# Block 1's attention contexts on tiles of 64 rows and 32 columns of the matmul array

## The chip, the core and the metric

The kernel runs on one NeuronCore of a Trainium2 chip. A core has five engines, each with a queue of its own that it works through in order: TensorE (PE, the 128x128 matmul array, whose results go to PSUM), VectorE (DVE), ScalarE (ACT), GpSimd (POOL) and SyncE (SP, which issues the DMAs here). PSUM has eight banks; a tile `[128, 512]` of float32 fills one. The metric is the time of one execution in microseconds (us), the median of several runs.

## What is computed

The input `x` has 32 sequences of 64 tokens with 512 channels. Two transformer blocks run one after the other, in float32:

```python
# block 0: 8 query heads of 64, 1 key/value head, rope, softmax over all 64 keys, gated MLP of 2048
x = res + ctx @ Wo.T
x = x + silu(h @ Wg.T) * (h @ Wu.T) @ Wd.T

# block 1: layer norm with scale and shift, 16 query heads of 32, 4 key/value heads from a latent of 128
q = (h @ Wq.T).reshape(B, T, 16, 32).transpose(0, 2, 1, 3)
c_kv = h @ Wkd.T
k = (c_kv @ Wku.T).reshape(B, T, 4, 32).transpose(0, 2, 1, 3)
v = (c_kv @ Wvu.T).reshape(B, T, 4, 32).transpose(0, 2, 1, 3)
k_exp = jnp.repeat(k, 4, axis=1)
v_exp = jnp.repeat(v, 4, axis=1)
attn = softmax(rope(q) @ rope(k_exp).T / sqrt(32))   # 64 tokens: the mask hides nothing
y = attn @ v_exp                                      # the "contexts" that the change rearranges
out = x + y.transpose(0, 2, 1, 3).reshape(B, T, 512) @ Wo.T
```

So in block 1 four query heads share one key/value head (a "group"), and there are four groups, numbered g = 0 to 3. In the kernel g = 2m + r, with m and r each 0 or 1.

## The kernel before

The 2048 tokens are cut into eight units of 256 tokens, four sequences each. A unit passes through block 0's attention (`attention0`), the MLP (`mlp`, with seven products in place of eight for each pair of 2x2 blocks), and block 1's attention (`attention1`). Generators stand for these, and `Order` interleaves their pieces: while TensorE works on the MLP of unit u, pieces of `attention0` of unit u+1 and `attention1` of unit u-1 are put between. Below that, the compiler's scheduler gives each engine its final order of instructions and gives each PSUM tile a bank, from the banks that it reckons to come free first. At the start (list `FIRST`) and at the end (list `LAST`) the order on TensorE is written out by hand. At the end nothing is left of the MLP, and `attention1` of the units 6 and 7 runs alone.

What the change touches lies in `attention1`:

- `keys_values` (L855 on) makes keys and values of the unit. The keys go to `kb` with a mask, twice for each sequence: in copy r only the channels of the group r of a pair stay, the rest is zero. The values of a sequence go to `vb` in block-diagonal form: rows 0 to 63 (the 64 keys) hold the 32 channels of r = 0, rows 64 to 127 hold those of r = 1 in the next 32 columns, and the rest is zero. Eight copies on ACT (L883) write them; the zeros were written once, by `early` (L1093) for the two buffers `vblk1`, and by a memset (L1204) for unit 7's own.
- `scores(t)` (two sequences at a time, t = 0 or 1) makes a bank of scores for each m, with the columns in the order (head j, copy r, key), on tiles of 64 rows and 64 columns of the array. `softmax` works on each bank, `turn` turns the result with TensorE transposes (`turned`, L600) and copies it to `pT` (L601, ACT).
- `context(t, pTs)` multiplies: for a sequence b of the two and a pair m, one matmul of all 128 rows (64 keys of r = 0 and 64 of r = 1) and 64 columns (32 channels of each), over 4 x 64 = 256 moving columns. Four such matmuls fill one bank, `cx`; two copies (L951 on ACT; for unit 7 the second on DVE, L949) bring it to `cT`, and `output` multiplies that by `wo1` (`po`, L565).

A float32 matmul shows in the trace as two matmul records. The products of the MLP are L977 (`gu`) and L1036 (`down`).

Of the kernel before, what the change touches and what calls it, by code (L numbers as in the profile page):

```python
# [17 lines left out]
P = 128  # L18
B, S, D = 32, 64, 512
T = B * S  # L20
KC = D // P
UT = 256
US = UT // S
# [5 lines left out]
HD1, HALF1 = 32, 16  # L29
# [15 lines left out]
TURN = (0.15911865234375, 3.628432750701904e-05, 6.4192136051133275e-09, 1.4247115856860781e-12)  # L45
ROUND = 12582912.0
WARM = 11
STAY = 14104
FIRST = "aaaaaaa bb a mm aa bb a bbb aa b mm a bb r aa a m b a bi m b i a | b".replace(" ", "")
EARLY = 4  # L50

# [1 line left out]
TWO_PI = float(np.nextafter(np.float32(2 * np.pi), np.float32(0)))  # L53


C_COND, C_VECS, C_CS1, C_MASK, C_FREQ = 0, KC * B, KC * B + 16, KC * B + 16 + 2 * S, KC * B + 18 + 2 * S
C_SIGN, C_ALL = C_FREQ + 1, C_FREQ + 2

OTHER = [(i + HALF1) % 32 for i in range(32)]
# [67 lines left out]
def two_blocks(ctx: ExitStack, tc: tile.TileContext, a: dict, out: bass.AP):  # L127
    nc = tc.nc
# [8 lines left out]
    def bank(tag, name):  # L137
        return psum.tile([P, 512], F32, tag=tag, name=name, bufs=BANKS[tag])
# [4 lines left out]
    def abank(name):  # L143
        tags = homes["now"]
        homes["n"] += 1
        return bank(tags[homes["n"] % len(tags)], name)


    stays = {"all": const.tile([P, STAY], F32, tag="stays", name="stays"), "at": 0}

    def fixed(shape):
        n, i = int(np.prod(shape[1:])), stays["at"]
        stays["at"] += n
        assert stays["at"] <= STAY
        t = stays["all"][:, i : i + n]
        if len(shape) == 2:
            return t
        names = "abc"[: len(shape) - 1]
        return t.rearrange(f"p ({' '.join(names)}) -> p {' '.join(names)}", **dict(zip(names, shape[1:])))

    def work(tag, shape, name, bufs=2):
        return wk.tile(shape, F32, tag=tag, name=name, bufs=bufs)
# [19 lines left out]
    for q in range(US):  # L182
        rows = slice(q * HALF0, (q + 1) * HALF0)
        for i in range(2):
            block = ident[rows, rows][:, i * HALF1 : (i + 1) * HALF1].unsqueeze(1).unsqueeze(1)
            to = spread[rows, q].rearrange("p (r a h f) -> p r a h f", r=2, a=2, h=2)[:, :, i]
# [24 lines left out]
    kmask = small[:, C_MASK:C_FREQ]  # L211
# [5 lines left out]

    vblk0 = [fixed([P, US, HD0]) for i in range(2)]

    vblk1 = [fixed([P, US, 2, 2 * HD1]) for i in range(2)]  # L220

    s0a = fixed([P, KC, B])
    s0b = fixed([P, KC, B])
# [225 lines left out]
    def tables_by_quarters(u, few, room):  # L449

        r = few[:, 0]
        nc.vector.tensor_tensor(
            few[:, 1:3], angle[:, :, u * S : (u + 1) * S], r.unsqueeze(1).to_broadcast([P, 2, S]), ALU.mult
        )
        ps = abank(f"tab_{u}").rearrange("p (i b s) -> p i b s", i=2, s=S)
        spread_out(ps, few[:, 1:3])
        pr = abank(f"row_{u}")[:, :UT]
        spread_out(pr.rearrange("p (b s) -> p b s", s=S), r)
        cs = work("cs", [P, 2, UT], f"cs_{u}", 1)
        ps = ps.rearrange("p i b s -> p i (b s)")  # L460
        nc.scalar.copy(cs[:, 0], ps[:, 0])
        nc.scalar.mul(cs[:, 1], ps[:, 1], sign_of)
        row = space(room, "r", UT, f"r_a{u}")
        nc.scalar.copy(row[HD0:], pr[HD0:])
        return cs[:, 0], cs[:, 1], row
# [22 lines left out]
    def tile4(room, tag, name):  # L488
        return space(room, tag, KC * UT, name).rearrange("p (c t) -> p c t", t=UT)
# [33 lines left out]
    def root_row(parts, eps, room, name):  # L523

        r = space(room, "r", UT, f"r_{name}")[:, :S]
        root_by_quarters(parts, eps, r, f"qs_{name}")
        yield 0.5, 1.0
        pr = abank(f"row_{name}")[:, :UT]
        spread_out(pr.rearrange("p (b s) -> p b s", s=S), r)
        return pr  # L530
# [94 lines left out]

    mlp_in = {}

    def attention0(u, room, early=None, late=None):
        kb, vb = kblk0[u % 2], vblk0[u % 2]
        lean = "lean" in room  # L630
        h = tile4(room, "h", f"h0_{u}")
# [14 lines left out]
        def keys_values():  # L646
            kv = abank(f"kv0_{u}")
            project(kv[:, :UT], wqkv[0], slice(2 * P, 3 * P), h)
            return kv

        norm = rms(u, s0a, h, room, f"a{u}")
        yield next(norm)
        if early:
            early()
        r = yield from norm
        kv, turn = None, None
        if lean:
            few = space(room, "few", 3 * S, f"quarters_{u}").rearrange("p (k c) -> p k c", c=S)
            if u == 0:

                idle(4)
                kv = keys_values()
            root_by_quarters(r, eps0, few[:, 0], f"ms_a{u}")
            kv = kv or keys_values()
# [4 lines left out]
        if lean:  # L669
            cos, sin, r = tables_by_quarters(u, few, room)  # L670
# [9 lines left out]
        kv = kv or keys_values()  # L680
# [36 lines left out]
        for ts in ((0,), (1,)) if lean else ((0, 1),):  # L717
            banks = [abank(f"sc0_{u}_{ts[0]}_{r}")[:, : 256 * len(ts)] for r in range(2)]
            for n in range(KC * len(ts)):
                t, c = ts[n // KC], n % KC  # L720
                for b in range(2):
                    cols = slice((2 * t + b) * S, (2 * t + b + 1) * S)
                    for r, sc in enumerate(banks):
# [5 lines left out]
                            start=True,  # L729
                            stop=True,  # L730
                        )
            p = ps[ts[0]] if lean else both
# [3 lines left out]
        cT = tile4(room, "h", f"cT0_{u}")  # L736
        pTs = []
# [34 lines left out]
        r = yield from rms(u, s0b, h, room, f"b{u}")  # L772
        if lean:
# [4 lines left out]
            r = abank(f"row_b{u}")[:, :UT]  # L778
# [14 lines left out]


    def attention1(u, room):
        vb = room.get("vb", vblk1[u % 2])
        x = x_units[u]
        lean = "lean" in room
        early = "early" in room
# [20 lines left out]
        if slim:  # L820
            r = yield from root_row(parts, eps1, room, f"c{u}")
        else:
            r = space(room, "r", UT, f"r_c{u}")
# [33 lines left out]
        def keys_values():  # L857
            kv = abank(f"kv1_{u}")
            nc.tensor.matmul(kv[:, :UT], wkv1[:, 0], latT, start=True, stop=True)
            for t in range(2):  # L860
                nc.tensor.matmul(
                    kv[:, UT + t * P : UT + (t + 1) * P], latT[:, t * P : (t + 1) * P], wkv1[:, 1], start=True, stop=True
                )
            kr = space(room, "kr", UT, f"kr_{u}").rearrange("p (b s) -> p b s", s=S)
            few = [P, US, S]
            rotate(
                kr,
                kv[:, :UT].rearrange("p (b s) -> p b s", s=S),
                cos.unsqueeze(1).to_broadcast(few),
                sin.unsqueeze(1).to_broadcast(few),  # L870
                few,
                f"k1_{u}",
            )
            kb = space(room, "kb", 2 * UT, f"kb1_{u}").rearrange("p (b g s) -> p b g s", b=US, g=2)
            wide = [P, US, 2, S]
            mask = kmask.unsqueeze(1).unsqueeze(3).to_broadcast(wide)
            nc.gpsimd.tensor_tensor(kb, kr.unsqueeze(2).to_broadcast(wide), mask, ALU.mult)
            for t in range(2):
                for b in range(2):
                    v = kv[b * S : (b + 1) * S, UT + t * P : UT + (t + 1) * P]  # L880
                    v = v.rearrange("p (m r d) -> p m r d", m=2, r=2)
                    for r in range(2):
                        nc.scalar.copy(  # L883
                            vb[r * S : (r + 1) * S, 2 * t + b, :, r * HD1 : (r + 1) * HD1], v[:, :, r, :]
                        )
            return kb

        queries = [query(i) for i in range(2)]
# [14 lines left out]
        cT = tile4(room, "h", f"cT1_{u}")  # L903
# [29 lines left out]
            return pTs  # L933

        def context(t, pTs):
            cx = abank(f"cx1_{u}_{t}").rearrange("p (b c s) -> p b c s", b=2, c=KC)
            for b in range(2):
                for m in range(2):
                    nc.tensor.matmul(  # L939
                        cx[m * S : (m + 1) * S, b],  # L940
                        vb[:, 2 * t + b, m, :],
                        pTs[m][:, :, b * S : (b + 1) * S],
                        start=True,
                        stop=True,
                    )
            to = cT[:, :, t * P : (t + 1) * P].rearrange("p c (b s) -> p b c s", s=S)
            for b in range(2):
                if slim and b:
                    nc.vector.tensor_copy(to[:, b], cx[:, b])  # L949
                else:  # L950
                    nc.scalar.copy(to[:, b], cx[:, b])  # L951

        ps = []
        for t in range(2):
# [3 lines left out]
            if not lean:  # L958
                pTs = yield from turn(t, ps[t])
                context(t, pTs)  # L960
                yield 1.0, 1.5 * t
        if lean:
            pTs = []
# [125 lines left out]
            if i == 1:  # L1089
                load_sets(MW)  # L1090

    def early():
        for z in vblk1:  # L1093
            nc.gpsimd.memset(z, 0.0)

    def second(u, room=None):
        room = room or {"ring": "1"}
        while u not in finished:
# [17 lines left out]
    first = work("p0", [P, 1024], "p0_0", 1)  # L1116

    def later_angles():
# [2 lines left out]

    ahead = Job(attention0(1, {"ring": "1", "lean": True}, late=later_angles), A0)
    streams = {
        "a": attention0(0, {"ring": "0", "lean": True, "p": [first[:, :512], first[:, 512:]]}, early),
        "b": ahead.pieces,
        "m": other_mods(),
    }
# [28 lines left out]
    def spare(tag, cols, name, bufs=2):  # L1156
        return work(tag, [P, cols], f"own_{name}", bufs)
# [5 lines left out]
        "ring": "0",  # L1163
        "lean": True,
        "early": True,
        "vb": vblk1[0],
        "p": [t[:, j * 512 : (j + 1) * 512] for t in two for j in range(2)],
        "latT": [few[:, :UT]],
        "kr": [few[:, UT:]],
# [15 lines left out]
    for u in range(NU):  # L1185
# [14 lines left out]
        rest = order.run(jobs, until=tuple(must))  # L1200
    order.run([*rest, Job(down(NU * NP - 1), 3.0)])
    homes["now"] = everywhere
    zeros = spare("pT1", 512, "vb7", 2).rearrange("p (b r d) -> p b r d", b=US, r=2)
    nc.gpsimd.memset(zeros, 0.0)  # L1204
    big = [spare("mw", 1792, f"mw{j}", MW) for j in range(4)]
    room7 = {
        "ring": "-",
        "lean": True,
        "vb": zeros,
        "h": [big[0][:, :1024], big[1][:, :1024], big[1][:, :1024]],  # L1210
        "latT": [big[0][:, 1024:1280]],
        "kr": [big[0][:, 1280:1536]],
# [95 lines left out]
```

## Time and profile before

| what | value |
|---|---|
| median of 3 runs | 1032.84 us (1032.0 to 1033.85) |
| the profiled execution | 1034.73 us, its span from first to last instruction 1032.7 us |
| mean granted TensorE clock | 0.996 |
| DVE, POOL, ACT busy | 547.4, 437.4, 332.2 us |
| block 1's contexts on TensorE (L939) | 128 records of 128 rows x 64 columns, 256 moving columns |
| block 0's contexts on TensorE (L746) | 128 records of 64 x 64, 256 moving columns |
| value copies to `vb` (L883, ACT) | 64 of 206 ns |
| memsets for the zeros (L1094, L1204, POOL) | 3 of 524 ns, at 1.8, 13.0 and 949.1 us |

A line of the timeline reads: start in us, duration in us, engine, source line, operation, out<-in, tile of the array (rows * columns), shape, number of records merged into the line. The duration of a merged line runs to the modelled end of its last record, which lies after the next line's start, because matmuls are pipelined. What a stretch takes of TensorE is therefore read from the start of one line to the start of the next.

### The profile page before, as it was taken

Reading aid. Unit: us, or ns where it says so; the run is one execution under the profiler, and the core shown is the slowest. Engines: PE = TensorE matmul, PEld = TensorE weight load, DVE = VectorE, ACT = ScalarE, POOL = GpSimd, SP = SyncE. Lnnn points to the kernel's source line nnn. Section 1 sums busy time; section 2 is a strip of 40 time slices with the busy share of each in tenths; the row PEclk is TensorE's granted clock in tenths of the full one; section 3 lists DMA queues with packets and bytes.
Section 4 is the critical chain, followed back from the end, with each engine's and each line's share of the span. In section 5 each row is a group of like instructions: output and inputs, shape, how many; then the busy total and the mean of one; then the engine's idle time right before and its main releaser. Section 6 shows DMA issues by size and latency. Waiting matters only on the chain.

```text
span 1032.7 us, 21599 instructions
## 1 busy us (share of the span) xinstructions
PE 1004.3 (97%) x8598; PEld 935.9 (91%) x8598; DVE 547.4 (53%) x1376; ACT 332.2 (32%) x684; POOL 437.4 (42%) x522
## 2 busy tenths in 40 slices
PE   8999899999999999999999999999999999999997
PEld 7789899998999988989999989899999899999986
DVE  5766855535355485343664366652565525553374
ACT  4432113345114243142340342242333522334042
POOL 5335446344254442345342454324563243643351
PEclk9999999999999999999999999999999999999999
DMA  9736896363665364672646646447754547666201
GB/s 322 260 128 227 269 328 242 116 215 128 235 214 203 122 224 151 217 259 101 235 149 228 235 143 213 156 149 240 247 182 161 186 166 258 215 215 215 92 1 41
DMA packets 68850, 198.53 MB, mean 192 GB/s; under 512 B 7312, under 2 KB 16272, under 8 KB 68368
## 3 DMA queue, kind: packets, MB, share of 16 engines
q1 hardware_dynamic: 68752, 197.17, 55.2%
q8 instruction: 68, 1.11, 0.4%
q14 instruction: 30, 0.25, 0.1%
HBM read 180.37 MB, written 16.78 MB: 191 GB/s over the span
## 4 chain that ended last, share of the span: by engine, by line
PE 84%; DVE 6%; POOL 4%; DMA 2%; issue 2%; ACT 1%; SPq 0%; POOLq 0%; DVEq 0%; ACTq 0%
PE gu L977 34%; PE down L1036 17%; PE q L565 11%; PE po L565 9%; PE sc L912 2%; PE pp L600 2%; PE cx L939 2%; PE lat L565 1%; DMA set<-in_wmlp 1%; PE kv L565 1%; PE sc L725 1%; PE cx L746 1%; PE tab L436 1%; DMA mod<-in_mod 1%; DVE sm L593 1%
## 5 line engine op out<-in xcount | busy, mean ns | idle before, releaser
L977 PE MATMUL gu<-h,set 128*128 128x128 f32 x2048 | 288.1, 277 | 10.2 <-DVE c L996 5.6
L977 PEld LDWEIGHTS gu<-h,set 128*128 128x128 f32 x2048 | 259.1, 192 | 19.3 <-issue 13.0
L977 PE MATMUL gu<-hc,set 128*128 128x128 f32 x1536 | 215.7, 276 | 0.0
L977 PEld LDWEIGHTS gu<-hc,set 128*128 128x128 f32 x1536 | 194.0, 193 | 1.1 <-issue 0.6
L1015 POOL TENSOR_TENSOR act<-c,c 128x384 f32<-128x384 f32 x64 | 66.5, 1039 | 198.2 <-DVE c L1003 141.8
L1036 PE MATMUL down<-td,set 128*128 128x128 f32 x1024 | 137.7, 276 | 2.5 <-POOL td L1018 2.5
L1036 PEld LDWEIGHTS down<-td,set 128*128 128x128 f32 x1024 | 125.6, 192 | 4.2 <-POOL td L1018 3.4
L989 ACT COPY e<-gu 128x128 f32<-128x128 f32 x128 | 33.7, 264 | 261.0 <-PE gu L977 246.9
L1003 DVE TENSOR_TENSOR c<-gu,u 128x256 f32<-128x256 f32 x128 | 53.4, 419 | 106.5 <-PE gu L977 106.0
L1036 PE MATMUL down<-act,set 128*128 128x128 f32 x768 | 109.6, 278 | 0.0
L565 PE MATMUL q<-h,stays 128*128 128x256 f32 x480 | 109.1, 380 | 0.0
L565 PE MATMUL po<-cT,stays 128*128 128x256 f32 x480 | 108.3, 380 | 0.7 <-ACT cT L756 0.7
L991 DVE TENSOR_TENSOR u<-e,gu 128x128 f32<-128x128 f32 x128 | 36.0, 281 | 129.9 <-ACT e L989 129.1
L1036 PEld LDWEIGHTS down<-act,set 128*128 128x128 f32 x768 | 97.8, 192 | 5.3 <-issue 3.2
L565 PEld LDWEIGHTS q<-h,stays 128*128 128x128 f32 x480 | 89.5, 190 | 12.1 <-issue 0.4
L565 PEld LDWEIGHTS po<-cT,stays 128*128 128x128 f32 x480 | 89.2, 190 | 12.0 <-ACT cT L756 0.8
L595 POOL TENSOR_TENSOR p<-p,sm 128x512 f32<-128x512 f32 x40 | 41.3, 1050 | 121.0 <-DVE sm L594 113.7
L576 POOL TENSOR_TENSOR qT<-u_q,v_q 128x512 f32<-128x512 f32 x30 | 38.1, 1270 | 85.8 <-DVE v_q L575 85.7
L1072 ACT ACT_TABLE_LOAD x35 | 44.9, 1283 | 54.9 <-DVE c L1003 54.4
L621 DVE TENSOR_TENSOR x<-x,po 128x512 f32<-128x512 f32 x28 | 19.2, 687 | 72.8 <-PE po L565 72.8
L1017 POOL TENSOR_TENSOR td<-act 128x256 f32<-128x256 f32 x64 | 46.8, 732 | 5.6 <-DVE act L1014 0.9
L1072 ACT ACTIVATE c<-gu 128x128 f32<-128x128 f32 x64 | 17.7, 277 | 86.2 <-DVE c L1003 82.4
(267 smaller groups left out, 1335.7 us busy)
## 6 DMA issues: line engine op xcount, KB each, us to landing
set<-sums SPq DMA_DIRECT2D x168, 512.0 KB, 5.5
set<-in_wmlp SPq DMA_DIRECT2D x192, 384.0 KB, 4.4
sums<-set SPq DMA_DIRECT2D x24, 512.0 KB, 4.4
x<-in_x SPq DMA_DIRECT2D x8, 512.0 KB, 6.4
mod<-in_mod SPq DMA_DIRECT2D x7, 512.0 KB, 7.1
a<-in_wmlp SPq DMA_DIRECT2D x24, 128.0 KB, 3.2
out_x<-x SPq DMA_DIRECT2D x12, 256.0 KB, 2.5
stays<-in_wo SPq DMA_DIRECT2D x2, 1024.0 KB, 10.8
```

What stands on the lines that cost most here:

```text
L565: nc.tensor.matmul(ps, w[:, k, cols], h[:, k, :], start=(k == 0), stop=(k == KC - 1))
L576: nc.gpsimd.tensor_tensor(dst, u, v, ALU.add)
L595: nc.gpsimd.tensor_tensor(p8, p8, sm.unsqueeze(2).to_broadcast(wide), ALU.mult)
L600: nc.tensor.transpose(pp[:, c, :], p[:, c * P : (c + 1) * P], ident)
L977: nc.tensor.matmul(ps, w[:, slot, k * P : (k + 1) * P], b[of][:, k], start=start and k == 0, stop=k == 1, skip_group_check=True)
L989: nc.scalar.copy(e, ps[:, 0])
L991: nc.vector.tensor_tensor(u2, e, ps[:, 1], ALU.add)
L1003: nc.vector.tensor_tensor(c.rearrange("p (a b) t -> p a b t", b=2)[:, :, 1], ps[:, 2:4], u2.unsqueeze(1).to_broadcast([P, 2, HT]), ALU.add,)
L1015: nc.gpsimd.tensor_tensor(act[:, 1:4], gate[:, 1:4], c[:, 1:4], ALU.mult)
L1017: nc.gpsimd.tensor_tensor(td[:, 0:2], act[:, 1:3], act[:, 0:2], ALU.subtract)
L1036: nc.tensor.matmul(sums_of[u][p][:, c], w[:, slot, c * P : (c + 1) * P], b[of], start=q % NP == 0 and i % 2 == 0 and c == 0, stop=q % NP = ...
L1072: nc.scalar.activation(gate[2][:, 0], gate[0][:, 0], AF.Silu)
```

## The change

The values lose their zeros. `vb` of a sequence has 32 columns for each m, and its 128 rows hold r = 0 and r = 1: in the order (0, 1) for the sequence b = 0, and (1, 0) for b = 1. The mask of the keys gets the same turn, so that the keys' copies of each second sequence stand in the order (1, 0). A context is then one matmul for each sequence, m and r: 64 rows (the half where this r lies) and 32 columns (at position 32 g). There are eight in place of four for a t, on eight different tiles of the array, and each sequence has a bank of its own. The copies to `vb` are four in place of eight, each of 64 x 128 elements. Three memsets go, and so does unit 7's own buffer.

```diff
-    vblk1 = [fixed([P, US, 2, 2 * HD1]) for i in range(2)]
+    vblk1 = [fixed([P, US, 2, HD1]) for i in range(2)]
...
-        vb = room.get("vb", vblk1[u % 2])
+        vb = vblk1[u % 2]
...
-            mask = kmask.unsqueeze(1).unsqueeze(3).to_broadcast(wide)
+            mask = kmask.rearrange("p (b g) -> p b g", g=2).unsqueeze(3).to_broadcast(wide)
             nc.gpsimd.tensor_tensor(kb, kr.unsqueeze(2).to_broadcast(wide), mask, ALU.mult)
-            for t in range(2):
-                for b in range(2):
-                    v = kv[b * S : (b + 1) * S, UT + t * P : UT + (t + 1) * P]
-                    v = v.rearrange("p (m r d) -> p m r d", m=2, r=2)
-                    for r in range(2):
-                        nc.scalar.copy(
-                            vb[r * S : (r + 1) * S, 2 * t + b, :, r * HD1 : (r + 1) * HD1], v[:, :, r, :]
-                        )
+            v = kv[:, UT:].rearrange("p (t m r d) -> p t m r d", t=2, m=2, r=2)
+            for b in range(2):
+                for r in range(2):
+                    rows = slice((r ^ b) * S, (r ^ b) * S + S)
+                    nc.scalar.copy(
+                        vb.rearrange("p (t b) m d -> p b t m d", b=2)[rows, b], v[b * S : (b + 1) * S, :, :, r]
+                    )
...
         def context(t, pTs):
-            cx = abank(f"cx1_{u}_{t}").rearrange("p (b c s) -> p b c s", b=2, c=KC)
-            for b in range(2):
-                for m in range(2):
-                    nc.tensor.matmul(
-                        cx[m * S : (m + 1) * S, b],
-                        vb[:, 2 * t + b, m, :],
-                        pTs[m][:, :, b * S : (b + 1) * S],
-                        start=True,
-                        stop=True,
-                    )
-            to = cT[:, :, t * P : (t + 1) * P].rearrange("p c (b s) -> p b c s", s=S)
-            for b in range(2):
+            banks = [abank(f"cx1_{u}_{t}_{b}")[:, :UT].rearrange("p (c s) -> p c s", s=S) for b in range(2)]
+            for m in range(2):
+                for r in range(2):
+                    for b, cx in enumerate(banks):
+                        rows, g = slice((r ^ b) * S, (r ^ b) * S + S), 2 * m + r
+                        nc.tensor.matmul(
+                            cx[g * HD1 : (g + 1) * HD1],
+                            vb[rows, 2 * t + b, m],
+                            pTs[m][rows, :, b * S : (b + 1) * S],
+                            start=True,
+                            stop=True,
+                        )
+            for b, cx in enumerate(banks):
+                to = cT[:, :, t * P + b * S : t * P + (b + 1) * S]
                 if slim and b:
-                    nc.vector.tensor_copy(to[:, b], cx[:, b])
+                    nc.vector.tensor_copy(to, cx)
                 else:
-                    nc.scalar.copy(to[:, b], cx[:, b])
...
-    def early():
-        for z in vblk1:
-            nc.gpsimd.memset(z, 0.0)
...
-    zeros = spare("pT1", 512, "vb7", 2).rearrange("p (b r d) -> p b r d", b=US, r=2)
-    nc.gpsimd.memset(zeros, 0.0)
...
-    mask = (np.arange(P)[:, None] % 64 // HD1 == np.arange(2)).astype(np.float32)
+    mask = (np.arange(P)[:, None] % 64 // HD1 == np.array([0, 1, 1, 0] * 2)).astype(np.float32)
```

## The prediction, made before the changed kernel ran

> **What bounds the kernel now.** I read the page's head and busy times first: TensorE is busy in nearly all of the span, at full clock, and no other engine passes 53%.
>
> ```profile
> span 1032.7 us, 21599 instructions
> PE 1004.3 (97%) x8598; PEld 935.9 (91%) x8598; DVE 547.4 (53%) x1376; ACT 332.2 (32%) x684; POOL 437.4 (42%) x522
> PE 84%; DVE 6%; POOL 4%; DMA 2%; issue 2%; ACT 1%; SPq 0%; POOLq 0%; DVEq 0%; ACTq 0%
> ```
>
> The third line is the chain of waits: 84% of the span is TensorE's own work. So a microsecond less on TensorE is a microsecond less of time, except in stretches where TensorE waits. From the sums by stretch, TensorE idles 5.8 us of 220 in 200–420, 3.3 of 240 in 420–660, 0.1 of 170 in 660–830, 1.25 of 155 in 830–985. Next, the timeline of TensorE around a context of block 1 and a context of block 0:
>
> ```profile
> 394.04 1.08 PE L939 MATMUL cx<-pT,stays 128*64 128x256 f32 x8
> 395.05 0.71 PE L977 MATMUL gu<-h,set 128*128 128x128 f32 x4
> ...
> 336.56 1.09 PE L746 MATMUL cx<-pT,stays 64*64 64x256 f32 x16
> 337.59 0.71 PE L1036 MATMUL down<-act,set 128*128 128x128 f32 x4
> ```
>
> From start to next start, block 1's eight records take 1.01 us and block 0's sixteen take 1.03. All stream 256 columns; a full-array record of that width takes 0.216 us (the groups' `po` L565, 16 records in 3.46 us). So records on different tiles run side by side: eight on two tiles are four waves, sixteen on four tiles also four. A context costs 0.15 + 0.216 per wave. Unit 6 agrees: sixteen records on two tiles, eight waves, run from 1005.40 to the next line at 1007.31: 1.91 us, against 0.15 + 8 x 0.216 = 1.88. In one wave the single starts lie 7 ns apart.
>
> **The change: contexts.** Now sixteen records go to eight tiles. If all eight run side by side: two waves, 0.15 + 2 x 0.216 + 6 more starts of 7 ns = 0.62 us, 0.39 less. The trace shows no eight at once. It shows two row halves with two column groups (L746 above), and one row group with four column groups (L330, 32 records of 128 columns from 27.79, first three pitches 7, 6, 7 ns, waves of 109 ns). Both at once is new, and so is a bank written from both row halves: block 0 gives each row half its own bank. Bounds: two waves (-0.39), or one record after another, sixteen waves, 3.6 us (+2.6). I take two waves: neither four column streams nor two row halves slowed a wave in those rows, and the two halves write different partitions of the bank.
>
> [...]
>
> Places, by the order in which the changed program's instructions stand on TensorE. Eight contexts of units 0 to 5 stand whole: 8 x -0.39 = -3.1. The second contexts of units 2 and 4 are cut into two runs of four, a bank each, with `down` products between: 2 x (0.15 + 0.43 + 0.02) + 0.10 for one more change of tiling (a first tiled record starts 0.205 after the last full one, a usual pitch is 0.112) = 1.30 against 1.01: +0.29 each, +0.6. The first contexts of units 3 and 4 were cut before (0.58 + 1.01) and are cut into two and six matmuls now (0.58 + 0.62): -0.39 each, -0.8. Sum -3.3.
>
> **Scores get another order.** They take 1.03 us when the two banks alternate, more when one bank's matmuls come first:
>
> ```profile
> 362.69 1.10 PE L912 MATMUL sc<-kb,qT 64*64 64x128 f32 x32
> 363.72 1.05 PE L1036 MATMUL down<-act,set 128*128 128x128 f32 x7
> ...
> 811.06 1.09 PE L912 MATMUL sc<-kb,qT 64*64 64x128 f32 x16
> 812.08 0.71 PE L1036 MATMUL down<-act,set 128*128 128x128 f32 x4
> 812.63 0.39 PE L1036 MATMUL down<-td,set 128*128 128x128 f32 x2
> 812.94 1.09 PE L912 MATMUL sc<-kb,qT 64*64 64x128 f32 x16
> 813.96 0.49 PE L1036 MATMUL down<-td,set 128*128 128x128 f32 x2
> ...
> 685.61 1.97 PE L725 MATMUL sc<-stays,qT 64*64 64x64 f32 x64
> 687.50 0.71 PE L1036 MATMUL down<-act,set 128*128 128x128 f32 x4
> ```
>
> Unit 4's second scores stand as two halves (1.02 + 1.02); in the changed program they alternate: -1.0. Block 0's scores of unit 6 (1.89) alternate after four; with the alternating price of 1.09 (L725 at 318.96), 0.1 for another change of tiling and 0.28 for the second bank (the two copies from `cx` at 377.11 start 0.27 apart): 1.47, -0.4. In units 1, 2 and 5 (1.30 before) two `gu` products now stand between contexts and scores, and both score banks are just-used context banks (unit 2 excepted): 1.03 + 0.28 + 0.1, about 0, from -0.2 to +0.3 each. Sum -1.4.
>
> **New waits.** A context takes two banks, so scores wait for two ACT copies in place of fewer. A copy starts 0.04 after the context's last modelled end (377.07) and takes 0.38; the last record starts 0.32 after the first and lasts 0.38. So the banks are free about 1.1 and 1.4 us after the context's start. TensorE, at 0.62, first does two `gu` products (four records, 0.54 with the tiling change): 1.15, just covered for the first bank. Behind a waiting score stands all of TensorE's queue. ACT idled 1.17 us before those copies, so I add nothing; without that cover a table load (1.28) in front costs that much in each of three places.
>
> **Where gains are lost.** In unit 1 DVE is back to back from 376 to 390 with angles and softmax, and TensorE waits for it:
>
> ```profile
> 386.08 0.44 PE L600 MATMUL pp<-stays,p 128*128 128x128 f32 x2 [0.81 <-POOL p L595]
> 388.32 1.13 PE L977 MATMUL gu<-h,set 128*128 128x128 f32 x8 [1.80 <-DVE c L996]
> ```
>
> What the context at 375.94 saves becomes a longer wait here: 0.4 lost, and I allow 0.2 more for the other waiting stretch (602, 1.67 us). +0.6.
>
> **The tail.** Nothing covers it:
>
> ```profile
> 1020.63 0.37 ACT L951 COPY own_mw<-cx 128x256 f32<-128x256 f32 x1 [0.49 <-PE cx L939]
> 1021.04 0.42 DVE L949 COPY own_mw<-cx 128x256 f32<-128x256 f32 x1 [3.44 <-ACT own_mw L951]
> 1021.44 0.37 ACT L951 COPY own_mw<-cx 128x256 f32<-128x256 f32 x1 [0.44 <-PE cx L939]
> 1021.85 0.42 DVE L949 COPY own_mw<-cx 128x256 f32<-128x256 f32 x1 [0.38 <-ACT own_mw L951]
> 1022.33 7.17 PE L565 MATMUL po<-own_mw,stays 128*128 128x256 f32 x32 [0.93 <-DVE own_mw L949]
> ```
>
> The DVE copy of the same bank waits for ACT's. With two banks the program lets it wait for TensorE alone. Unit 7: contexts start at 1019.45; the last `pT` copy ends at 1020.14, so the last four matmuls run from 1020.20, their second records start by 1020.50 and end by 1020.87; both copies run from 0.10 after, to 1021.40; `po` starts at 1021.46: -0.87. Unit 6: its last `pT` lands at 1006.25, so the last records start by 1006.53 and scores at 1006.84, not 1007.31: -0.47. Sum -1.3.
>
> **The rest costs nothing.** Value copies on ACT: eight of 206 ns become four of about 260 (between 206 for 64x64 and 366 for 64x256): -0.6 us of ACT per unit, where ACT idles two thirds; the queue behind gains nothing on the path. The memsets at 1.8 and 13.0 lie under TensorE's waits for DMA and for products of POOL that end before 13.0; the one at 949.1 is followed by no wait of TensorE. The key mask keeps its shape, 128x512; no DMA is added.
>
> **Sum.** -3.3 - 1.4 + 0.6 - 1.3 = -5.4 us. The profiled execution took 1034.73 in all, 2.0 of it outside its span of 1032.7; the median is 1032.84, near this span, and I take the difference from the median: 1027.4. Bounds of this case: the losses could double and the scores bring nothing (1029.8), or nothing is lost and units 1, 2, 5 gain 0.2 each (1026.2); with half a microsecond of run-to-run spread, 1025.7 to 1030.3.
>
> **Rivals.**
> (1) The change doesn't do what it says: four at once, each row half and bank apart. Whole contexts keep four waves (0), runs of four in one bank take four waves each (2 x (2 x 1.01 + 0.1 - 1.01) = +2.2), the two that were cut +0.2 each, scores -1.4, parallel copies in the tail -0.4: about 1033.7. For it: no row shows a bank shared by row halves. Against: the different partitions.
> (2) Slower: in each context a matmul that meets a busy bank holds the queue, so only two run at once. Eight waves, 1.88 us, +0.87 for each of sixteen contexts: +13.9; the scores' -1.4 and the copies' -0.4 stay: 1044.9. It decides from six waves per context on (16 x 0.43 = +6.9, against -1.8). For it: in the scores at 213.18 five matmuls of one bank ran in pairs before those of the other bank began, though on other rows. Against: in unit 0's context at 233.00 one column group went on while the other still waited for its `pT`.
> (3) The waits for the two banks: table loads or MLP copies on ACT stand before the context copies, about 1.3 us in three places: 1031.3. For it: ACT is in order, and a table load came right after the copies at 377.77. Against: the idle 1.17 us.
>
> **How the numbers follow.** The forecast gets 0.68, rival (1) 0.09, rival (2) 0.13, rival (3) 0.10. What a measurement can tell from no change is about 0.2%, 2.1 us: faster means under 1030.8. The forecast lies there, and (3) about half: faster 0.73. Same: (1) and the rest of (3): 0.13. Slower: (2), and (1) if a little worse: 0.14. The forecast's own range would hold under 0.6; it is carried over (3) and (1): 1025.0 to 1033.8.
>
> **What would show it.** Right: contexts of sixteen records in 0.62 us from start to next start, starts 7 ns apart eight at a time; unit 4's second scores at 1.03; in the tail ACT and DVE copies side by side and `po` about 0.9 us sooner after the contexts' start; TensorE's waits at 386 and 388 longer. Wrong: contexts of 1.0 us (rival 1) or 1.9 (rival 2); waits of scores for ACT `cT` (rival 3). A slower loop of DVE or POOL in the MLP, which I do not expect, would also break the sum.

## The result, and the profile after

| | kernel before | changed kernel |
|---|---|---|
| median | 1032.53 us (1030.47 to 1034.56, 6 runs) | 1026.80 us (1025.15 to 1028.28, 6 runs) |
| ratio of the times | | 0.9939, 95% interval 0.9926 to 0.9952 |
| profiled execution, span | 1034.73, 1032.7 us | 1028.28, 1026.3 us |
| contexts of block 1 (L939), start to the next kind's start, summed | 18.43 us | 13.08 us |
| scores of block 1, summed likewise | 20.75 us | 19.65 us |
| scores of block 0, summed likewise | 12.65 us | 12.32 us |
| all gaps of TensorE after its first instruction | 24.1 us | 22.0 us |

The change saves 5.7 us in the medians, 6.3 by the ratio (0.0061 x 1032.5). A second set of five runs (experiment 10) gave 0.9933 (0.9920 to 0.9946).

The head of the page of the changed kernel and, as the third line, the shares of its chain of waits:

```profile
span 1026.3 us, 21720 instructions
PE 999.9 (97%) x8726; PEld 931.3 (91%) x8726; DVE 551.1 (54%) x1376; ACT 327.3 (32%) x652; POOL 436.0 (42%) x519
PE 84%; DVE 7%; DMA 3%; POOL 3%; ACT 2%; issue 1%; SPq 0%; POOLq 0%; DVEq 0%; ACTq 0%
```

TensorE still sets the end. It has 128 records more and 4.4 us less of busy time. The timeline of TensorE around a context, around unit 4's second scores and around block 0's scores of unit 6 (in the changed file the scores are L909 and L723, the context is L939 as before):

```profile
392.29 0.66 PE L939 MATMUL cx<-pT,stays 64*32 64x256 f32 x16
392.88 0.71 PE L977 MATMUL gu<-h,set 128*128 128x128 f32 x4
...
682.44 1.36 PE L723 MATMUL sc<-stays,qT 64*64 64x64 f32 x64
683.73 0.49 PE L1036 MATMUL down<-td,set 128*128 128x128 f32 x2
...
808.30 1.10 PE L909 MATMUL sc<-kb,qT 64*64 64x128 f32 x32
809.33 0.49 PE L977 MATMUL gu<-hc,set 128*128 128x128 f32 x2
```

Start to start, the context takes 0.593 us where it took 1.014. Inside it, eight records start 6 to 7 ns apart, 194 ns pass, and eight more start 6 to 7 ns apart: eight tiles at once, two waves (a wave is what runs on different tiles side by side). Unit 4's second scores are one run of 1.03 us where there were two of 1.02, and block 0's scores of unit 6 take 1.30 us where they took 1.89. Those of unit 5 went the other way, from 1.72 to 1.93, which the sum for block 0 in the table includes.

The tail, unit 7's contexts up to the output product:

```profile
1013.83 1.38 PE L939 MATMUL cx<-own_mw,stays 64*32 64x256 f32 x32
...
1014.58 0.37 ACT L951 COPY own_mw<-cx 128x256 f32<-128x256 f32 x1
1014.62 0.42 DVE L949 COPY own_mw<-cx 128x256 f32<-128x256 f32 x1 [2.62 <-PE cx L939]
1015.26 0.37 ACT L951 COPY own_mw<-cx 128x256 f32<-128x256 f32 x1 [0.31 <-PE cx L939]
1015.30 0.42 DVE L949 COPY own_mw<-cx 128x256 f32<-128x256 f32 x1 [0.25 <-PE cx L939]
1015.87 1.32 PE L565 MATMUL po<-own_mw,stays 128*128 128x256 f32 x5 [0.66 <-DVE own_mw L949]
```

The copies on ACT and DVE now run side by side, each waiting for TensorE alone. From the contexts' start to `po` 2.05 us pass, where 2.88 did.

Not all went as smoothly. TensorE's waits in unit 1, and three stretches as sums (columns: stretch in us, length, then busy time of PE, PEld, DVE, ACT and POOL with their instructions, the granted clock, DMA share and GB/s), first the kernel before, then the changed one:

```profile
236.00:252.00 16.00, 14.08 (x131) 13.38 (x130) 8.13 (x18) 7.98 (x12) 7.44 (x10) 0.89 0.46 173
370.00:400.00 30.00, 27.22 (x240) 24.80 (x239) 21.48 (x61) 11.92 (x25) 9.21 (x12) 1.00 0.56 193
590.00:610.00 20.00, 18.01 (x139) 16.82 (x138) 9.78 (x18) 9.60 (x14) 12.74 (x12) 1.00 0.45 155
```

```profile
236.00:252.00 16.00, 14.78 (x157) 13.96 (x163) 10.88 (x26) 8.27 (x13) 7.02 (x9) 1.00 0.50 174
370.00:400.00 30.00, 26.86 (x236) 24.70 (x234) 21.04 (x60) 10.62 (x24) 8.53 (x10) 0.89 0.34 124
590.00:610.00 20.00, 19.82 (x159) 19.14 (x158) 11.93 (x21) 9.62 (x14) 15.05 (x13) 1.00 0.37 130
```

```profile
382.50 0.55 PE L600 MATMUL pp<-stays,p 128*128 128x128 f32 x3 [1.84 <-POOL p L595]
384.34 2.05 PE L977 MATMUL gu<-h,set 128*128 128x128 f32 x8 [1.29 <-DVE c L996]
```

The wait in the third stretch (1.67 us at 602) is gone and the one in the first is shorter (1.92 us at 245.75, now 1.22 at 244.10). In unit 1 the waits grew from 0.81 + 1.80 to 1.84 + 1.29 us. The granted clock moved too: the column with 0.89 stands in the first stretch before and in the second after. In the clock's own record it is 0.5 for 3.41 us from 247.16 before, and for 6.83 us from 383.31 after. The records of TensorE show it too: in the changed kernel the MLP's products start 0.213 us apart between 384.9 and 390, and 0.112 us apart between 391 and 396 (medians).

### The profile page after: what moved, and what is told of

Read it like the earlier page. It is cut to its first block, busy times and chain, and to the rows that moved or that the text cites. A ratio compares the mean times of both kernels' runs of the same rounds, so it can differ in the third digit from the quotient of the medians.

```text
span 1026.3 us, 21720 instructions
## 1 busy us (share of the span) xinstructions
PE 999.9 (97%) x8726; PEld 931.3 (91%) x8726; DVE 551.1 (54%) x1376; ACT 327.3 (32%) x652; POOL 436.0 (42%) x519
## 4 chain that ended last, share of the span: by engine, by line
PE 84%; DVE 7%; DMA 3%; POOL 3%; ACT 2%; issue 1%; SPq 0%; POOLq 0%; DVEq 0%; ACTq 0%
PE gu L977 34%; PE down L1036 17%; PE q L565 11%; PE po L565 10%; DMA set<-in_wmlp 2%; PE pp L600 2%; PE sc L909 1%; PE lat L565 1%; PE kv L565 1%; PE cx L939 1%; PE sc L723 1%; PE cx L744 1%; DVE sm L593 1%; DMA stays<-in_wqkv 1%; PE tab L436 1%
## 5 line engine op out<-in xcount | busy, mean ns | idle before, releaser
L1003 DVE TENSOR_TENSOR c<-gu,u 128x256 f32<-128x256 f32 x128 | 53.4, 419 | 109.6 <-PE gu L977 109.1
```

What stands on the lines that cost most here:

```text
L1003: nc.vector.tensor_tensor(c.rearrange("p (a b) t -> p a b t", b=2)[:, :, 1], ps[:, 2:4], u2.unsqueeze(1).to_broadcast([P, 2, HT]), ALU.add,)
```

## The experiments

All times are medians. Each ratio, with its 95% interval, is to the kernel before, run on the same chip in the same set; it is estimated from all runs and is not the quotient of the medians. The changed kernel's own time is that of the result above unless experiment 10 is named, so distances to it go across sets. The kernel before had 1033.38 us in the first set (experiments 1 to 4), 1034.14 in the second (5, 6), 1034.17 in the third (7 to 9) and 1033.91 in the last (10, 11).

**1. Two banks alone.** The kernel before, with the accumulation of each sequence in a bank of its own:

```diff
-            cx = abank(f"cx1_{u}_{t}").rearrange("p (b c s) -> p b c s", b=2, c=KC)
-            for b in range(2):
+            banks = [abank(f"cx1_{u}_{t}_{b}")[:, :UT].rearrange("p (c s) -> p c s", s=S) for b in range(2)]
+            for b, cx in enumerate(banks):
                 for m in range(2):
                     nc.tensor.matmul(
-                        cx[m * S : (m + 1) * S, b],
+                        cx[m * S : (m + 1) * S],
...
-            to = cT[:, :, t * P : (t + 1) * P].rearrange("p c (b s) -> p b c s", s=S)
-            for b in range(2):
+            for b, cx in enumerate(banks):
+                to = cT[:, :, t * P + b * S : t * P + (b + 1) * S]
                 if slim and b:
-                    nc.vector.tensor_copy(to[:, b], cx[:, b])
+                    nc.vector.tensor_copy(to, cx)
                 else:
-                    nc.scalar.copy(to[:, b], cx[:, b])
+                    nc.scalar.copy(to, cx)
```

> The kernel before, with one part of the change alone: each sequence's context has a PSUM bank of its own, the four matmuls of 128 rows by 64 columns and the zeros in the values stay. Theory (the gain is the number of tiles that run at once): a whole context stays at 1.01 us from start to next start; what is left of the gain is unit 4's second scores (-1.0), some of block 0's scores of unit 6 (-0.4) and parallel copies in the tail (-0.4), less two contexts cut in two (+0.25 each): -0.5 to -2 us against before, ratio 0.998 to 0.9995. Rival (the gain comes from the banks, the order of the scores and the copies): most of the 6 us, ratio 0.994 to 0.996.

Measured: 1033.63 us, ratio 1.0000 (0.9985 to 1.0014). TensorE's timeline, a whole context and one that is cut:

```profile
392.66 1.08 PE L939 MATMUL cx<-pT,stays 128*64 128x256 f32 x8
393.68 0.71 PE L977 MATMUL gu<-h,set 128*128 128x128 f32 x4
...
534.26 0.65 PE L939 MATMUL cx<-pT,stays 128*64 128x256 f32 x4
534.84 0.71 PE L1036 MATMUL down<-act,set 128*128 128x128 f32 x4
535.39 0.39 PE L1036 MATMUL down<-td,set 128*128 128x128 f32 x2
535.71 0.65 PE L939 MATMUL cx<-pT,stays 128*64 128x256 f32 x4
```

Whole contexts stay at 1.01, their sum at 18.43 us. The scores of both blocks lose 2.08 us in all, and the tail's last contexts 0.31. Still the profiled span is only 1.2 us shorter, and no difference shows in the runs: the two cut contexts cost 0.15 each, and the MLP's products, between which more tiled products now stand, take 1.0 us more (with gaps and half-clock stretches taken off). Banks, order and copies alone bring next to nothing, a little less than the theory had. The rival falls.

**2. Four tiles in place of eight.** The changed kernel with both sequences' groups in the same order:

```diff
-                    rows = slice((r ^ b) * S, (r ^ b) * S + S)
+                    rows = slice(r * S, r * S + S)
...
-                        rows, g = slice((r ^ b) * S, (r ^ b) * S + S), 2 * m + r
+                        rows, g = slice(r * S, r * S + S), 2 * m + r
...
-    mask = (np.arange(P)[:, None] % 64 // HD1 == np.array([0, 1, 1, 0] * 2)).astype(np.float32)
+    mask = (np.arange(P)[:, None] % 64 // HD1 == np.array([0, 1] * 4)).astype(np.float32)
```

> The changed kernel, but both sequences have their groups in the same order (r in place of r xor b), so that a context's eight matmuls lie on four tiles of 64 x 32 and not on eight; instructions, banks and their order on TensorE are those of the changed kernel. Theory: two tiles' worth of streams less at once, four waves: a whole context 1.03 us in place of 0.59, the ones that are cut in two runs of four keep 0.57 each; some eleven whole contexts lose 0.43, so about 5 us of the gain go: ratio 0.9975 to 0.9995 against before. Rival (the eight tiles do not matter, since a row half serves its matmuls one after another or the order does the work): contexts stay at 0.59 or the time stays at that of the changed kernel, ratio 0.994.

Measured: 1031.07 us, ratio 0.9983 (0.9970 to 0.9996), 4.3 us above the changed kernel.

```profile
391.18 1.09 PE L939 MATMUL cx<-pT,stays 64*32 64x256 f32 x16
392.20 0.71 PE L977 MATMUL gu<-h,set 128*128 128x128 f32 x4
```

The same sixteen records now take 1.02 us, in four waves of four, each from both row halves; the contexts sum to 18.36 us, 5.27 more than in the changed kernel. The theory holds in time and ratio: the number of tiles at once is most of what the change is worth. A bank written from both row halves costs nothing here either, since 1.02 is the price of four waves (0.15 + 4 x 0.216).

**3. Twice the matmuls.** `for m in range(2)` in `context` becomes `for m in [0, 1] * 2`.

> The changed kernel with every context matmul issued twice (the second writes the same values again): two waves more per context, 0.43 us, 16 contexts. Theory (a microsecond of TensorE is a microsecond of time): +6.9 us against the changed kernel, ratio about 1.000 to 1.001 against before. Rival (TensorE's waits in unit 1's softmax stretch and the tail take up part of what a context costs or saves): +3 to +5 us, ratio 0.997 to 0.999.

Measured: 1033.43 us, ratio 1.0002 (0.9990 to 1.0014), 6.6 us above the changed kernel. The contexts sum to 19.75 us, 6.67 more than there.

```profile
518.68 1.09 PE L939 MATMUL cx<-pT,stays 64*32 64x256 f32 x32
519.71 0.71 PE L977 MATMUL gu<-h,set 128*128 128x128 f32 x4
```

Thirty-two records on eight tiles are four waves, 1.02 us. So a microsecond on TensorE here is a microsecond of time, as the theory had it, within what the runs can tell. The rival with 3 to 5 us falls.

**4. The angles sooner.** In unit 1 DVE works on the rope angles of the units 4 and 5 among the softmax. The call moves from the end of `attention0` to just before its output product:

```diff
             contexts([0, 1])
             yield 1.1, 2.5
+            if late:
+                late()
...
-        if late:
+        if late and lean:
             late()
```

> The changed kernel with the angles of the units 4 to 7 computed before block 0's output product instead of after the norm behind it, so that DVE does them some 30 us sooner, away from the softmax of block 1 that they now stand between; TensorE's order changes in four lines. Theory (in unit 1 the saving is lost because DVE, full of angles and softmax, makes TensorE wait 1.8 and 1.3 us near 382 to 384, and the clock granted afterwards is 0.5 for 6.8 us): both waits shrink below 0.5 us, no stretch of half clock follows, 3 to 6.5 us are won: ratio 0.988 to 0.991 against before. Rival (the waits come from the chain softmax, POOL, transposes itself, angles or not): within 1 us of the changed kernel, ratio 0.993 to 0.995.

Measured: 1027.92 us, ratio 0.9947 (0.9929 to 0.9964). The theory's gain did not come. DVE, POOL and TensorE in the new place:

```profile
353.25 1.84 DVE L378 TENSOR_SCALAR stays<-stays 128x128 f32<-128x128 f32 x1
355.12 1.25 DVE L379 TENSOR_TENSOR prod<-stays 128x128 f32<-128x128 f32 x1
356.41 0.70 DVE L393 TENSOR_SCALAR ang<-prod 128x128 f32<-128x128 f32 x1
357.14 0.23 DVE L378 TENSOR_SCALAR stays<-ang 128x128 f32<-128x128 f32 x1
```

```profile
353.09 1.91 POOL L552 TENSOR_TENSOR h<-x,stays 128x1024 f32<-128x1024 f32 x1 [2.91 <-DVE x L621]
354.96 1.26 POOL L494 TENSOR_TENSOR sq_b<-sq_b 128x512 f32<-128x512 f32 x1
356.30 0.72 POOL L495 TENSOR_TENSOR tot_b<-sq_b 128x256 f32<-128x256 f32 x1
```

```profile
360.52 1.83 PE L979 MATMUL gu<-h,set 128*128 128x128 f32 x7 [5.09 <-DVE c L998]
```

```profile
357.73 0.31 ACT L395 ACTIVATE stays<-ang 128x128 f32<-128x128 f32 x1 [3.56 <-DVE ang L379]
358.14 1.04 ACT L539 ACTIVATE sq_a<-x 128x1024 f32<-128x1024 f32 x1
359.09 0.41 ACT L991 COPY e<-gu 128x128 f32<-128x128 f32 x2
```

Both waits in unit 1 are gone, so they did hang on the angles and the rival's cause falls too, though its ratio (0.993 to 0.995) came true; but one wait of 5.09 us stands at 360, and 6.83 us of half clock follow from 358.3. Each stretched DVE instruction ends 0.09 to 0.15 us after the POOL instruction beside it (355.09 and 355.00, 356.37 and 356.22, 357.11 and 357.02), while the same lines take 0.23 to 0.29 us when POOL is idle (357.14). The three take 3.0 us more beside POOL; what holds DVE there is not shown. The MLP's `c` stood behind them by two ways: behind the angles in DVE's order, and behind ACT, which idled 3.56 us for the last angle before its sines, and made the copies `e` for `c` only after these and a square of 1.04 us. In unit 1 of the changed kernel it is the same: L379 takes 1.09 us at 382.90 beside POOL's `p` (382.81 to 383.85), and the next instruction on DVE is the `c` that TensorE awaits until 384.34.

**5 and 6. The angles in seven pieces over the unit**, on the changed kernel (5) and on the one before (6). `angles` becomes a generator with a `yield 0.0, 12.0` after its beginning and after each of the five products, and is a job of its own beside the MLP:

```diff
-            turn = (lambda u=u: angles(u + 2)) if u % 2 == 0 and u + 2 < NU else None
-            must.append(Job(attention0(u + 1, {"ring": "0"}, late=turn), A0))
+            must.append(Job(attention0(u + 1, {"ring": "0"}), A0))
+            if u % 2 == 0 and u + 2 < NU:
+                must.append(Job(angles(u + 2)))
```

> The changed kernel with the angles of the units 4 to 7 cut into seven pieces (one to begin, five for the products, one to end) that are spread over the unit in which they are due, in place of one block; the sign of the positions is computed a second time for the last piece. In the order of DVE's instructions the pieces now stand between other work of block 0's attention, two to four instructions at a time. Theory (experiment 4 only moved the block of angles in front of another step of the MLP, where TensorE then waited 5.1 us; the waits belong to the block, not to unit 1): the waits of 1.84 and 1.29 us near 382 and 384 go, none over 1 us takes their place between 300 and 420, and the clock stays full there; 3 to 6.5 us less than the changed kernel, ratio 0.988 to 0.991 against before. Rival (DVE is full from 300 to 390 in any order, so the wait only goes elsewhere again): within 1.5 us of the changed kernel, ratio 0.992 to 0.996.

> The kernel before with the same spread of the angles, and none of the change. Theory (part of what the change saves was eaten in unit 1 by longer waits and by half-clock stretches after them): the distance from this kernel to the changed kernel with the spread is larger than the 6.3 us between the changed kernel and the one before: 7 to 8 us; this kernel itself gains about 2.5 us from its own waits in unit 1 (0.8 and 1.8 us): ratio 0.996 to 0.998 against before. Rival (nothing was eaten): the distance stays at 5.5 to 6.5 us.

Measured: 1026.62 us, ratio 0.9931 (0.9910 to 0.9952), for 5; 1031.96, ratio 0.9985 (0.9968 to 1.0003), for 6. The scheduler put most of the pieces close together again, and the last of them next to POOL's norm, in experiment 5:

```profile
303.84 1.27 POOL L501 TENSOR_TENSOR sq<-sq 128x512 f32<-128x512 f32 x1 [0.99 <-ACT sq L821]
303.95 1.30 DVE L379 TENSOR_TENSOR prod_last<-stays 128x128 f32<-128x128 f32 x1
305.06 1.96 POOL L823 TENSOR_TENSOR h<-h,stays 128x1024 f32<-128x1024 f32 x1
305.37 1.73 DVE L400 TENSOR_SCALAR ang<-prod_last 128x128 f32<-128x128 f32 x1
```

TensorE waits 2.99 us at 308.13 for `c`; in experiment 6, 2.98 at 311.58. So the theory of 5 fails as that of 4 did, for the same cause at a third place. The theory of 6 fails too: its kernel gained less than foretold (0.9985, where 0.996 to 0.998 was expected), and the two kernels lie 5.3 us apart (5.6 by the ratios), nearer to the rival's 5.5 to 6.5 than to 7 to 8. Since each carries a wait of 3 us, this tells little of unit 1.

**7, 8 and 9. Nine pieces, each behind the first products of an MLP step.** There the MLP has nothing for DVE until the last products: in the changed kernel's trace, from the end of each step's second `c` (L996) to the next L1003, 64 stretches of 192 us in all, DVE is busy for 47% and POOL for 21%, where the whole span has 54% and 42%. On the changed kernel for the units 4 to 7 (7), for the units 2 to 7 (8), and on the kernel before for the units 4 to 7 (9):

```diff
             up = first_products(1, q)
+            if q in (15, 31):
+                slot.append(angles(q // NP + 3))
+            if slot:
+                with after(tc, mybir.EngineType.DVE, latest(tc, mybir.EngineType.DVE)):
+                    if next(slot[0], True):
+                        slot.pop()
```

> The changed kernel with the angles of the units 4 to 7 in nine pieces, each put behind the last DVE instruction of an MLP step's first products, where DVE is idle next; the sign of the positions is computed a second time. Theory (the angles' DVE instructions, all operands in SBUF, are stretched from 0.23 to 0.29 us to 0.9 to 1.84 us while a POOL instruction runs, seen at 295.4, 303.95, 305.37 in experiment 5, and the MLP's next step, c, stands behind them; behind the first products POOL has little to do): no wait of TensorE over 1 us between 250 and 420, no stretch of half clock there, 3 to 5 us less than the changed kernel, 1022 to 1024 us, ratio 0.989 to 0.992 against before. Rival (any place costs TensorE 3 us, as three places did): 1026 to 1028 us, ratio 0.993 to 0.995.

> As experiment 7, with the angles of the units 2 and 3 in such pieces too, in the MLP of unit 0, in place of a block at about 103 us. Theory: the waits of TensorE of 1.4 and 1.5 us near 103 and 115 us go as well, 1.5 to 3 us less than experiment 7. Rival (in unit 0 DVE also adds up the weights and POOL is busy, so the pieces stretch there): within 1 us of experiment 7, or above it.

> The kernel before with the angles as in experiment 7, none of the change. It gives the change's distance with unit 1's disturbance gone on both sides. Theory (TensorE's saving of 5.35 us in the contexts and 1.4 in the scores passes whole into the time where no wait takes it): 6.5 to 7.5 us above experiment 7. Rival (part of the saving is taken by waits elsewhere, as with the spread angles, where the distance was 5.3): 5 to 6 us above it.

The pieces are those of experiment 5, with the beginning and the end cut in two each. Measured: 1023.83 us, ratio 0.9910 (0.9893 to 0.9927), for 7; 1026.95, ratio 0.9935 (0.9918 to 0.9951), for 8; 1030.77, ratio 0.9967 (0.9954 to 0.9981), for 9. Sums by stretch in unit 1, the changed kernel first, then experiment 7 (columns as above):

```profile
376.00:383.00 7.00, 5.16 (x45) 4.77 (x43) 6.90 (x24) 4.02 (x6) 1.23 (x2) 1.00 1.00 378
383.00:387.00 4.00, 2.71 (x13) 2.69 (x13) 2.82 (x10) 0.00 (x0) 0.85 (x1) 0.54 0.14 56
387.00:391.00 4.00, 4.00 (x25) 4.00 (x24) 2.14 (x7) 2.09 (x6) 0.59 (x1) 0.61 0.01 4
```

```profile
376.00:383.00 7.00, 7.00 (x72) 6.83 (x63) 6.76 (x18) 4.13 (x6) 1.87 (x4) 1.00 0.48 190
383.00:387.00 4.00, 3.60 (x33) 3.37 (x32) 2.70 (x9) 2.38 (x5) 0.87 (x1) 1.00 0.76 251
387.00:391.00 4.00, 4.00 (x47) 3.47 (x47) 0.87 (x4) 1.98 (x6) 2.63 (x4) 1.00 0.94 348
```

Of the angle instructions on DVE after 200 us, 11 of 70 last over 0.45 us in the changed kernel, 17 of 76 in experiment 5 and 6 of 76 in experiment 7; beside each of them a POOL instruction runs. In the changed kernel the 54 of the 70 that no POOL instruction overlaps take 0.30 us at most.

In unit 1 TensorE's busy time is nearly whole (14.6 of 15 us, where it had 11.9), its clock full, and no wait above 0.5 us is left between 250 and 420. That is the theory of 7, with its time. Experiments 7 and 9 lie 6.9 us apart in the medians, as the theory of 9 has it, but 5.9 by the ratios, as its rival has it: these runs don't tell the two apart. In the two traces TensorE's saving is whole: the contexts differ by 5.34 us, the scores by 1.18 and 0.38, 6.9 in all, and the gaps by less than 0.1. The profiled spans still differ by 5.3 only, and experiment 7's has one stretch of 3.41 us at half clock more, worth 1.7. Experiment 8 goes to its rival: the wait near 103 goes, but there are new ones of 0.8 us at 77 and of 1.6 at 93, where DVE is also adding up weights, and it is 3.1 us slower than experiment 7.

**10 and 11. The changed kernel and experiment 7 side by side**, both as they were.

> The changed kernel as it is, on the same chip as experiment 11, since experiment 7 and the changed kernel were timed apart. Theory and rival alike: 0.993 to 0.995 against before, 1026 to 1028 us.

> The kernel of experiment 7 again, beside the changed kernel. Theory (the waits near 382 to 384 and the half clock behind them are gone for good): 2.5 to 4.5 us below experiment 10. Rival (1023.8 in experiment 7 was the luck of a few executions, since half-clock stretches fall by chance): less than 1.5 us below it.

Measured: 1027.04 us, ratio 0.9933 (0.9920 to 0.9946), for 10; 1025.15, ratio 0.9923 (0.9909 to 0.9936), for 11. The difference is 1.9 us in the medians, between theory and rival, and 1.0 by the ratios, within the rival; across the first sets it was 3.0. The pieces seem to help, by 1 to 3 us, but the intervals of 10 and 11 overlap, so this is not shown for good. Experiment 7's kernel is the best one found.

**Not tried:** both sequences' contexts in one bank. There two row halves would write the same partitions of a bank with nothing to order them. What that does stays open, and so does the whole change with each row half in banks of its own.

## Why the prediction was right, point by point

The forecast was 1027.4 us, the median is 1026.8.

- **Contexts** (foretold 0.62 us, two waves, starts 7 ns apart): 0.593, two waves, 6 to 7 ns. The cost of 0.15 + 0.216 per wave gives 0.58. Experiments 2 and 3 show it at four waves with two other arrangements, 1.02 each. The first contexts of units 3 and 4 fell by 0.44 and 0.45 (foretold 0.39), and the cut second contexts of units 2 and 4 take 2 x 0.57 against 1.01, +0.12 without the change of tiling between their runs (foretold +0.29 with 0.10 for that). For the units 0 to 5 the sum is -4.1 where the prediction had -3.3: a whole context saved 0.42 and not 0.39, and the cuts cost less.
- **A bank written from both row halves** (foretold to slow no wave, since the halves write different partitions): at 0.593 us for two waves, eight records run at once, four in each bank, from both row halves. For row halves that write the same partitions no run here shows anything.
- **Scores' order** (foretold -1.4): -1.10 in block 1 (foretold -1.0) and -0.33 in block 0 (foretold -0.4), with unit 4's second scores at 1.03. The second figure is near by luck: unit 6 gained 0.60, and units 5 and 7, for which nothing was foretold, lost 0.21 and 0.06. The scores behind contexts in units 1, 2 and 5 stayed within 0.07 us of what they were.
- **New waits** (foretold 0): the two copies of unit 1's first context end at 373.07, 1.46 us after its start (foretold 1.4); scores begin at 372.86, behind the two `gu` products, and take 1.28, as before. The cover was just enough for the first bank, as foretold. Rival (3) falls; so do rival (1) by 0.593 and rival (2), which asked for 1.9 us.
- **Tail** (foretold -0.87 for unit 7, -0.47 for unit 6): -0.83 and -0.44.
- **Where gains are lost** (foretold +0.6): this step was off in its parts. Unit 1's waits grew by 0.5 us, as foretold. But at 602, where 0.2 more was allowed, 1.67 us vanished, and the wait at 245.75 shrank by 0.7, while one of 0.82 came at 528. In sum TensorE's gaps fell by 2.1 us. Against that stands what the prediction, which took TensorE to run at full clock, did not see at all: the clock. A stretch of 3.41 us at half clock costs 1.7 us of TensorE's work, and the changed kernel's profiled execution has one more than the other's (before the tail, 3.41 + 6.83 against 3.41 + 3.41). It falls in unit 1, where the lead over the kernel before shrinks from 4.33 us at the first context (1.7 of them the other's half clock at 247) to 1.75 at the second. In the profile of experiment 10, the same kernel again, the waits named here differ by at most 0.01 us, but unit 1 has half clock for 3.41 us only, and the mean clock is 0.997 where the changed kernel's first profile has 0.995: this cost changes from one execution to the next.
- **The bounds**: by its own terms the prediction's upper case is 1027.4 + 0.6 + 1.4 = 1029.4, not 1029.8. The measured 1026.8 lies within either.

Taken without the gaps inside them, the contexts, with those of the tail, make -5.1, the scores -1.4, all gaps of TensorE -2.1 and the clock +1.7: -6.9, against -6.4 between the profiled spans. The 0.5 left is not accounted for; the MLP's products take 0.8 us more than before (with gaps and half-clock stretches taken off), much as in experiment 1, and why is not tested. So the mechanism is right, and that the sum came so near is in part luck: it took the contexts' saving too small and left out both the shorter waits and the clock, which have opposite signs.

## What to carry to other kernels

Small products cost waves here, not instructions (sixteen records take 0.593 us on eight tiles and 1.02 on four): count how many different tiles of the array run at once, and split a product with padding zeros into twice as many on half-sized tiles if that fills the array. Two row halves that write different partitions of one bank slowed nothing here (the 0.593 us are with both halves in each bank); the same partitions were not tried. On this kernel, bound by TensorE, most or all of such a saving passes into the time (5.9 to 6.9 us of 6.9 between experiments 7 and 9), except where another engine's block of work stands in front of the next product. Such a block did best here behind the first products of an MLP step, where DVE and POOL are busy for 47% and 21% of the time (experiment 7, with no wait above 0.5 us between 250 and 420); moved whole, or cut finely but left to the scheduler, it made TensorE wait 3 to 5 us at a new place.

## What the runs showed of the hardware that was not expected

**Half clock followed short waits, by the grid on which they fell.** In the clock's record of each of the 13 profiles the granted share changes only at points that lie whole multiples of 3.413 us apart (in the changed kernel at 11.26, 14.67, 383.31 and 390.14 us: 1, 108 and 2 of them between one and the next). I summed TensorE's idle time in each such window, from the record's first point to TensorE's last matmul (matmul ends are modelled, so to about 0.1 us):

| window | next window | windows | idle time in the window |
|---|---|---|---|
| full clock | half clock | 20 | 1.92 to 2.92 us, one of 1.67 |
| full clock | full clock | 3830 | 1.75 us at most |
| half clock | full clock | 20 | 0.55 us at most |
| half clock | half clock | 3 | 0.86, 1.03, 2.18 us |

So in these traces about half a window of idle time is enough (the first two rows overlap between 1.67 and 1.75), and it can come from two waits, such as the 1.84 and 1.29 us of unit 1 (2.1 us of them in one window). The same wait may or may not do it. Experiments 7 and 11 are one kernel, and TensorE waits 1.93 us until 244.0 and until 244.3 in them; in 7 the wait lies within one window and 3.41 us of half clock follow from 244.89, in 11 the window's edge cuts it to 1.75 and none follow. The stretch from 244 on, first experiment 7, then 11:

```profile
244.00:248.00 4.00, 3.97 (x22) 3.98 (x23) 2.04 (x2) 0.94 (x3) 3.56 (x5) 0.61 0.96 386
```

```profile
244.00:248.00 4.00, 3.73 (x33) 3.73 (x34) 2.04 (x2) 1.19 (x3) 3.77 (x6) 1.00 1.01 391
```

It also goes with the spread of the runs. In the first set, the kernel before has a mean span of 1028.9 us in the five executions with a mean clock of 1.000, 1030.7 in the twelve with 0.998 and 1032.7 in the five with 0.995: 3.41 us at half clock take 0.0017 off the mean clock and, where TensorE is busy, put 1.7 us on the time. The first step fits that; the second, of two such stretches by the clock, is too small for it, and why is not shown. On this kernel a difference of a few us between two profiles should be compared with the clock first.
